# Moving one of the three softmax-sum additions of a layer-1 attention group from VectorE to an accumulating DMA issued by GpSimd

## Chip, cores and metric

The kernel runs on one core of one Trainium2 chip. The metric is the device time of one execution in microseconds (us). Three runs of the kernel before took 2781.45, 2784.82 and 2786.3 us; the median is 2784.82 us.

## What is computed

Two gated layers work on x of shape 8 x 512 x 256 with a context of 8 x 512 x 128. Each layer adds a gated attention part and a gated feed-forward part to x. The change touches the attention of layer 1, which has two blocks, a1 (self, with a mask on the normalised probabilities) and a2 (cross, on keys and values of the context):

```python
q = jnp.einsum('bsc,hcd->bhsd', xn, wq)      # H=16 heads, D=32
k = jnp.einsum('btc,hcd->bhtd', yn, wk)
v = jnp.einsum('btc,hcd->bhtd', yn, wv)
a = jax.nn.softmax(jnp.einsum('bhsd,bhtd->bhst', q, k) * D ** (-0.5), axis=-1)
if causal:
    mask = (jnp.arange(t)[None, :] > jnp.arange(s)[:, None]).astype(a.dtype)
    a = a * mask
o = jnp.einsum('bhst,bhtd->bhsd', a, v)
...
x_out = x + o @ li1_w + li1_b
h = jax.nn.gelu(_ln(x_out, ln3_g, ln3_b) @ li2_w + li2_b, approximate=False)
return x_out + h @ li3_w + li3_b
```

The softmax denominator runs over all 512 keys, also in block a1, since the mask comes after the softmax. All of this is in float32.

## The kernel before

Layer 0 fills about the first 920 us of the profile. After it, one woven section holds both attention blocks of layer 1 for all eight sequences, their MLPs (`mlp1`), the projections of queries and keys (`pair1`), the norms that enter a block (`pre1`, `enter1`), the last part of layer 0's feed-forward (`first`) and layer 1's feed-forward (`last`, `tail`).

**The attention steps.** `steps1` makes the list of one block: 4 groups `g` of 4 heads, and in each group 4 key tiles `n` of 128 keys. With 8 sequences and 2 blocks that is 64 groups and 256 steps. A step has two halves.

- `front(g, n)`: TensorE multiplies keys by queries into two PSUM tiles `ps_s`; ScalarE takes the exponential of both into one SBUF tile `pt` (128 keys x 4 heads x 512 queries, float32, 1 MB; L2217). In block a1 GpSimd makes a masked copy `dg` of the diagonal piece (L2221).
- `back(g, n)`: TensorE multiplies `pt` (and `dg`) by the values `vt` into the PSUM tile `ov`. For n = 1, VectorE makes `acc` = pt(0) + pt(1) (L2246). For n = 2, `acc` gets pt(2) as well (L2248). For n = 3, TensorE multiplies a matrix of ones by `acc` and by pt(3) into `sm`, which gives the denominators; VectorE turns them into reciprocals (`rt`, `recs`, `rb`, L2261 to L2264) and scales `ov` into `oT` (L2266).

`pt` has three buffers (`PTS = 3`), `acc` one, `dg` two, `ov` one. pt(n) of a group is freed when the additions and matmuls that read it are done; pt(2)'s buffer is next written by the front of n = 1 of the following group.

**The order.** `weave_all` merges the 256 steps with nine chains of other work. A front may be at most two ahead of the backs:

```python
if self.fronts < len(steps) and self.fronts - self.backs < 2:
```

A planner (`Pace`) keeps a model of when each engine is free and each tile is done, and `weave_all` emits the piece with the lowest place in the order among those that can start on TensorE within 0.3 us of the modelled present. The order is so fixed when the program is built; each engine then works through its own queue in that order. The back of n = 3 waits in the model until `acc` is done:

```python
return max(t, pace.when([Pace.name(st["acc"])]), pace.place("m1")) if n == NT - 1 else t
```

The model gives a two-input VectorE operation 0.15 us + 0.00106 us an element, so 2.3 us for `acc`. A DMA it models so (bytes n):

```python
self.free[e] = t0 + 0.4
self.wire = max(self.wire, t0 + 1.2) + n / 280e3
end = self.wire + 1.2
```

Where a piece can go to ScalarE or VectorE, `pace.sooner` chooses by the modelled load of the two.

Of the kernel before, what the change touches and what calls it, by code (L numbers as in the profile page):

```python
# [11 lines left out]
ALU = mybir.AluOpType  # L12
# [939 lines left out]
class Fast(General):  # L952
# [1238 lines left out]
    def steps1(self, b, blk):  # L2191
# [3 lines left out]
        nc, work, q, pace = self.nc, self.work, self.seqs[b], self.pace  # L2195
# [3 lines left out]
        st = {}  # L2199
# [29 lines left out]
        def back(g, n):  # L2229
            self.backs += 1  # L2230
            kt, pt, parts = st.pop((g, n))
            if n == 0:
                st["ov"] = self.ovp.tile([P, T], F32, tag="ov1", name="ov")
            ov = st["ov"]
            for i, (p, cols) in enumerate(parts):
                for j in (2, 3, 0, 1):
                    h = 4 * g + j
                    self.mm(
                        ov[32 * j : 32 * j + 32, cols], q["vt", blk][:, kt, 32 * h : 32 * h + 32],
                        p[:, j, : cols.stop - cols.start],  # L2240
                        n == 0 and i == 0, n == NT - 1 and i == len(parts) - 1,
                    )

            if n == 1:
                st["acc"] = work.tile([P, 4, T], F32, tag="acc", name="acc")
                nc.vector.tensor_tensor(st["acc"], st["pt"], pt, ALU.add)  # L2246
            elif n == 2:
                nc.vector.tensor_tensor(st["acc"], st["acc"], pt, ALU.add)  # L2248
            st["pt"] = pt
            if n < NT - 1:  # L2250
                return
            sm = self.bank()
            for k, t in enumerate((st["acc"], pt)):
                for j in (2, 3, 0, 1):
                    self.mm(sm[32 * j : 32 * j + 32, :], self.ones, t[:, j, :], k == 0, k == 1)

            if g == 0:
                st["recs"] = work.tile([P, 4, 16], F32, tag="recs", name="recs", bufs=2)
            rec = st["recs"][:, g, :]
            rt = work.tile([P, 16, 32], F32, tag="rt", name="rt", bufs=1)  # L2260
            nc.vector.transpose(rt.rearrange("p b d -> p (b d)"), sm)  # L2261
            nc.vector.reciprocal(rec, rt[:, :, 0])
            rb = work.tile([P, T], F32, tag="rt", name="rb", bufs=1)
            nc.vector.transpose(rb, rec.unsqueeze(2).to_broadcast([P, 16, 32]))  # L2264
            oT = q["oT", blk, g] = work.tile([P, T], F32, tag="oT", name="oT", bufs=5)
            nc.vector.tensor_tensor(oT, ov, rb, ALU.mult)  # L2266
            if g == 3:
                self.seen(st["recs"])

        def back_at(g, n):  # L2270
# [5 lines left out]
            if n == 0:  # L2276
# [3 lines left out]
        return [  # L2280
            (lambda g=g: front_at(g), lambda g=g, n=n: back_at(g, n),
             lambda g=g, n=n: front(g, n), lambda g=g, n=n: back(g, n))
            for g in range(4) for n in range(NT)
        ]
# [317 lines left out]
```

## Time and profile before

| | |
|---|---|
| median of three runs | 2784.82 us (2781.45 to 2786.3) |
| span of the profiled execution | 2779.7 us; the runs' median is 5.1 us more |
| mean granted TensorE clock | 0.959 |
| TensorE (PE) busy | 2517.8 us, 91% |
| VectorE (DVE) busy | 1736.5 us, 62% |
| ScalarE (ACT) busy | 1452.2 us, 52% |
| GpSimd (POOL) busy | 614.8 us, 22% |
| L2246, `acc` = pt(0) + pt(1) | 64 instructions, 149.2 us |
| L2248, `acc` += pt(2) | 64 instructions, 149.4 us |
| DMA queue of GpSimd | 2.62 MB in the whole program, none in layer 1's attention |

The time of the profiled execution itself is not given apart from its span, so the 5.1 us is taken for what lies around the span. In the profile a line such as `L2248 DVE TENSOR_TENSOR acc<-acc,pt` names the source line, the engine, the operation and the tiles written and read. `L1053` is the helper that records every matmul, so matmuls are told apart by their tiles: `ps_s` are the scores, `ov` the products with the values, `ps<-acc,ones` the first half of the denominators. "Idle before" is the time in which an engine stood still ahead of an instruction, with what released it. PEld is TensorE's weight load.

### The profile page before, as it was taken

What the parts mean: (1) busy time and instruction counts of PE and PEld (TensorE: products, weight loads), DVE (VectorE), ACT (ScalarE), POOL (GpSimd) and SP (SyncE); (2) the same over time, 40 slices, a digit from 0 to 9 for tenths busy, and PEclk for the clock granted to TensorE, in tenths of its full rate; (3) what the DMA queues carried; (4) which work ended last, traced back from release to release, by engine and by line L of the source; (5) the groups of instructions that cost most, each with busy time, mean ns of one, the idle gap of its engine ahead of it and who ended that gap; (6) DMA issues with size and microseconds to landing.
All of it is one profiled execution on the core that took longest, in us unless ns stands there. A gap on an engine that the chain in (4) does not pass through costs nothing.

```text
span 2779.7 us, 38478 instructions
## 1 busy us (share of the span) xinstructions
PE 2517.8 (91%) x15447; PEld 1223.8 (44%) x15452; DVE 1736.5 (62%) x3135; ACT 1452.2 (52%) x1803; POOL 614.8 (22%) x682
## 2 busy tenths in 40 slices
PE   7999999999786989999999999988999989999875
PEld 2333333333233344535554535545455454454554
DVE  4544554343476666564666777676777877767766
ACT  4666666656573554445444455444554555555421
POOL 2212222111001344231334231111114332101100
PEclk9999999999886999999999999999999999999987
DMA  3001120000364512211211013211021102211010
GB/s 113 25 27 50 50 73 16 20 31 12 118 261 173 178 46 99 80 46 42 76 60 63 16 54 107 69 38 58 24 82 60 43 4 89 71 45 43 23 38 17
DMA packets 76475, 176.55 MB, mean 64 GB/s; under 512 B 7424, under 2 KB 36480, under 8 KB 68992
## 3 DMA queue, kind: packets, MB, share of 16 engines
q1 hardware_dynamic: 73904, 170.81, 17.6%
q8 instruction: 123, 2.02, 0.3%
q0 software_dynamic: 800, 2.62, 0.3%
q10 hardware_dynamic: 1584, 0.58, 0.1%
q14 instruction: 64, 0.52, 0.1%
HBM read 111.07 MB, written 62.91 MB: 63 GB/s over the span
## 4 chain that ended last, share of the span: by engine, by line
PE 46%; DVE 13%; ACT 4%; POOL 2%; issue 2%; DMA 0%; ACTq 0%; POOLq 0%; DVEq 0%; SPq 0%
PE ps L1053 31%; PE ps_s L1053 8%; PE ov L1053 6%; ACT pt L2217 2%; PE ps L1056 1%; DVE hF L2332 1%; DVE acc L2246 1%; POOL dg L2221 1%; DVE rb L2264 1%; DVE hm L2342 1%; DVE z L144 1%; DVE mv L1971 1%; DVE rt L2261 1%; DVE oT L2266 1%; DVE acc L2248 1%
## 5 line engine op out<-in xcount | busy, mean ns | idle before, releaser
L2217 ACT ACTIVATE pt<-ps_s 128x1024 f32<-128x1024 f32 x512 | 496.3, 1021 | 418.0 <-PE ps_s L1053 313.6
L1053 PE MATMUL ps_s<-QT,KT 32*128 32x512 f32 (+3 forms) x4096 | 613.2, 607 | 28.3 <-ACT pt L2217 16.1
L1431 ACT ACTIVATE pt<-ps_s 128x1024 f32<-128x1024 f32 (+3 forms) x512 | 411.2, 862 | 202.6 <-PE ps_s L1053 194.3
L1053 PEld LDWEIGHTS ps_s<-QT,KT 32*128 32x128 f32 x4096 | 191.6, 184 | 368.0 <-issue 201.8
L1053 PE MATMUL ps<-x3T,li 128*128 128x256 f32 x1024 | 244.9, 391 | 3.9 <-DVE hp L2320 2.4
L1053 PE MATMUL ov<-pt,v 128*32 128x512 f32 (+3 forms) x2048 | 232.7, 525 | 13.5 <-POOL pt L1434 12.7
L1053 PE MATMUL ps<-li,hD 128*128 128x256 f32 x1024 | 239.1, 389 | 5.7 <-ACT hD L2164 5.7
L1053 PE MATMUL ov<-pt,vt 128*32 128x512 f32 (+3 forms) x1792 | 204.4, 526 | 36.2 <-DVE oT L2266 29.4
L1977 POOL TENSOR_SCALAR mv<-mv 128x2 f32<-128x2 f32 (+1 forms) x105 | 57.7, 550 | 770.4 <-DVE mv L1972 735.3
L2221 POOL TENSOR_SCALAR_AFFINE_SELECT dg<-pt 128x512 f32<-128x512 f32 x128 | 116.1, 908 | 505.6 <-ACT pt L2217 505.4
L1053 PEld LDWEIGHTS ps<-x3T,li 128*128 128x128 f32 x1024 | 192.5, 194 | 60.7 <-issue 18.4
L1053 PEld LDWEIGHTS ps<-li,hD 128*128 128x128 f32 x1024 | 193.8, 194 | 56.4 <-issue 14.5
L1434 POOL TENSOR_SCALAR_AFFINE_SELECT pt<-pt 128x512 f32<-128x512 f32 x128 | 86.3, 674 | 471.7 <-ACT pt L1431 470.0
L2248 DVE TENSOR_TENSOR acc<-acc,pt 128x2048 f32<-128x2048 f32 x64 | 149.4, 2334 | 4.3 <-ACT pt L2217 3.2
L2246 DVE TENSOR_TENSOR acc<-pt 128x2048 f32<-128x2048 f32 x64 | 149.2, 2332 | 1.1 <-ACT pt L2217 1.1
L1456 DVE STREAM_TRANSPOSE ot<-ov 128x512 f32<-128x512 f32 x64 | 45.8, 716 | 165.9 <-PE ov L1053 165.9
L2332 DVE SCALAR_TENSOR_TENSOR hF<-hp,cols,hF 128x256 f32<-128x256 f32 x224 | 114.6, 512 | 41.7 <-ACT hF L2323 35.6
L1053 PE MATMUL ps<-zT,a_wq 128*128 128x512 f32 x256 | 127.8, 623 | 2.1 <-DVE zT L2058 2.1
L1053 PE MATMUL ps<-li,oT 128*128 128x256 f32 x512 | 128.0, 394 | 1.7 <-DVE oT L2266 1.0
L1759 ACT ACTIVATE hD<-ps,cols 128x256 f32<-128x256 f32 x123 | 54.7, 471 | 137.1 <-PE ps L1053 100.5
L1053 PEld LDWEIGHTS ov<-pt,v 128*32 128x32 f32 x2048 | 40.4, 108 | 167.1 <-issue 100.2
L1053 PEld LDWEIGHTS ps<-li,oT 128*128 128x128 f32 x512 | 92.9, 191 | 47.7 <-issue 16.1
(305 smaller groups left out, 3654.9 us busy)
## 6 DMA issues: line engine op xcount, KB each, us to landing
hd<-h SPq DMA_DIRECT2D x16, 1024.0 KB, 3.9
hF<-hd SPq DMA_DIRECT2D x16, 1024.0 KB, 6.7
li<-in_w_a_dram SPq DMA_DIRECT2D x12, 1024.0 KB, 5.0
fw<-q_f_w SPq DMA_DIRECT2D x22, 512.0 KB, 5.5
xF<-xd SPq DMA_DIRECT2D x22, 512.0 KB, 5.1
kd<-k SPq DMA_DIRECT2D x8, 1024.0 KB, 3.9
vd<-v SPq DMA_DIRECT2D x8, 1024.0 KB, 5.2
res<-rd SPq DMA_DIRECT2D x32, 256.0 KB, 2.8
```

The costliest lines, as they stand in the source:

```text
L144: self.nc.vector.tensor_scalar(out[:, i, :], x[:, i, :], mv[:, i, 0:1], rstd[:, i : i + 1], ALU.subtract, ALU.mult,)
L1053: self.nc.tensor.matmul(out, lhsT, rhs, start=start, stop=stop, skip_group_check=True)
L1431: nc.scalar.activation(pt[:, 2 * jp : 2 * jp + 2, lo:], pss[jp][:, :, lo:], AF.Exp)
L1434: nc.gpsimd.affine_select(out=diag, in_=diag, compare_op=ALU.is_ge, fill=0.0, base=0, pattern=[[0, 4], [1, P]], channel_multiplier=-1,)
L1456: nc.vector.transpose(ot.rearrange("p b d -> p (b d)"), ov)
L1759: self.nc.scalar.activation(out, ps, AF.Identity, bias=bias)
L1977: nc.gpsimd.tensor_scalar(rstd, mv[:, :, 1], EPS, None, ALU.add)
L2217: nc.scalar.activation(pt[:, 2 * jp : 2 * jp + 2, :], pss[jp], AF.Exp)
L2221: nc.gpsimd.affine_select(out=dg, in_=pt[:, :, diag], compare_op=ALU.is_gt, fill=0.0, base=0, pattern=[[0, 4], [-1, P]], channel_multiplier=1,
L2246: nc.vector.tensor_tensor(st["acc"], st["pt"], pt, ALU.add)
L2248: nc.vector.tensor_tensor(st["acc"], st["acc"], pt, ALU.add)
L2332: nc.vector.scalar_tensor_tensor(a, hp[:, half + k : half + k + n], self.col("conv_w", 3 * f + k), a, ALU.mult, ALU.add)
```

## The change

For n = 2 the addition on VectorE is replaced by a DMA that GpSimd issues; it reads `pt`, adds it to `acc` in SBUF and writes `acc`. Nothing else is edited, and the planner, which models the new instruction as a DMA, orders the section anew.

```diff
--- before.py
+++ after.py
@@ -2245,7 +2245,7 @@
                 st["acc"] = work.tile([P, 4, T], F32, tag="acc", name="acc")
                 nc.vector.tensor_tensor(st["acc"], st["pt"], pt, ALU.add)
             elif n == 2:
-                nc.vector.tensor_tensor(st["acc"], st["acc"], pt, ALU.add)
+                nc.gpsimd.dma_start(st["acc"], pt, accum_op=ALU.add)
             st["pt"] = pt
             if n < NT - 1:
                 return
```

## Prediction

> **What bounds the kernel now.** I read the busy shares first, then the chain, then the stage that the change touches, then single groups. The page:
>
> ```profile
> PE 2517.8 (91%) x15447; PEld 1223.8 (44%) x15452; DVE 1736.5 (62%) x3135; ACT 1452.2 (52%) x1803; POOL 614.8 (22%) x682
> PE 46%; DVE 13%; ACT 4%; POOL 2%; issue 2%; DMA 0%; ACTq 0%; POOLq 0%; DVEq 0%; SPq 0%
> L2248 DVE TENSOR_TENSOR acc<-acc,pt 128x2048 f32<-128x2048 f32 x64 | 149.4, 2334 | 4.3 <-ACT pt L2217 3.2
> ```
>
> TensorE is the busiest engine and has the largest share of the chain; VectorE is second. The row of the edited line says that 64 additions of 2.33 us are removed. From the windows view, the stage that holds all 64 groups:
>
> ```profile
> core 0: us, PE busy (x) PEld busy (x) DVE busy (x) ACT busy (x) POOL busy (x), PEclk, DMA share, GB/s
> 925.00:2615.00 1690.00, 1581.01 (x9758) 827.60 (x9754) 1167.25 (x1997) 848.61 (x1000) 440.33 (x446) 0.97 0.18 59
> ```
>
> Of 1690 us TensorE is idle for 109. So emptying VectorE can bring at most these 109 us, and each microsecond that TensorE waits anew is to be paid unless it takes the place of a wait already there. The average group has 1690 / 64 = 26.4 us. The chain in this stage gives L2248 1.0% (17 us), L2246 1.8%, and `dg` 1.6% (27 us). What TensorE and ScalarE wait for, from the waits view of the stage:
>
> ```profile
> PE ov L1053 <- DVE oT L2266: 29.4, 18, 4.9
> PE ps L1053 <- DVE acc L2248: 4.7, 3, 2.3
> ACT pt L2217 <- DVE acc L2246: 56.1, 28, 4.9
> ```
>
> L2248 itself stops TensorE little (4.7 us). ScalarE's 56 us are for L2246, which frees pt(0) and stays. Then how soon the sum is needed, in one pressed group of the timeline:
>
> ```profile
> 976.01 2.29 DVE L2246 TENSOR_TENSOR acc<-pt 128x2048 f32<-128x2048 f32 x1 [0.58 <-ACT pt L2217]
> 976.11 2.69 POOL L2221 TENSOR_SCALAR_AFFINE_SELECT dg<-pt 128x512 f32<-128x512 f32 x1 [2.50 <-ACT pt L2217]
> ...
> 983.92 2.28 DVE L2248 TENSOR_TENSOR acc<-acc,pt 128x2048 f32<-128x2048 f32 x1
> ...
> 986.26 1.94 PE L1053 MATMUL ps<-acc,ones 128*32 128x512 f32 x8 [2.32 <-DVE acc L2248]
> ```
>
> The `acc` matmul starts 0.06 us after L2248 ends and TensorE stood idle 2.32 us for it. I took two distances from the timeline for all 64 groups. From the end of L2248 to the first `acc` matmul: median 3.9 us, below 1.1 us in 16 groups. From the end of L2246, when the new transfer could start at the earliest (pt(2) is mostly done by then), to that matmul: median 9.9 us, 20 groups below 7.0, 30 below 8.8, 40 below 12.0.
>
> **What the Trainium skill says.** "DMA: Bandwidth & Descriptors", section "Anatomy of one DMA — SWDGE (gpsimd) path", prices a GpSimd DMA at 2.0 us + bytes/436e3, thus 4.4 us for a plain 1 MB. The trace is slower: its only GpSimd loads of 256 KB took 4.3 us where this gives 2.6. I use the trace. The same page, section "Rules for kernel authors", says that an accumulating DMA reads its destination and writes it later; no page gives a rate for that, and nothing in this trace shows one. "SBUF — State Buffer", section "Who interferes with whom", says that a VectorE instruction with two SBUF inputs blocks a GpSimd instruction that reads SBUF. The trace agrees: the `dg` above started 0.1 us into L2246 and took 2.69 us, against a median of 0.635.
>
> **The change, part by part.** *Removed:* 64 x 2.334 = 149.4 us of VectorE. Most lies beside TensorE's work. On the path there were 17 us of L2248 itself. GpSimd's blocking by L2248 goes too: the 128 `dg` are 908 ns on average against 635, half of the surplus put to L2248 (the other half to L2246), so 27 us x 0.273/0.908 / 2 = 4 us. Together 21, taken as **20 us of gain**. Bounds: 0 (something else in VectorE's queue, such as `z`, is late next) and 40 (the reciprocals behind L2248, L2261 to L2266, move up as well).
>
> *Added: a transfer's latency.* The nearest rows:
>
> ```profile
> hd<-h SPq DMA_DIRECT2D x16, 1024.0 KB, 3.9
> vt<-vd SPq DMA_DIRECT2D x8, 1024.0 KB, 4.8
> rd<-res SPq DMA_DIRECT2D x16, 256.0 KB, 2.0
> res<-rd SPq DMA_DIRECT2D x32, 256.0 KB, 2.8
> cT<-cd POOLq DMA_DIRECT2D x8, 256.0 KB, 4.3
> ```
>
> Between 256 KB and 1 MB lie 1.9 to 2.0 us, so 1 MB moves in about 2.6. A plain 1 MB from GpSimd would land 4.3 + 1.9 = 6.2 us after issue. Reading the destination as well adds 2.6: **8.8 us is my value**, 5.2 of it data and 3.6 fixed. Bounds: 5.0 (the fastest `cT` load, 3.1, plus 1.9, the second read hidden) and 14.0 (the adding halves the data rate again: 3.6 + 10.4).
>
> *Where it falls.* The planner knows the transfer: 1.2 + 1,048,576/280e3 + 1.2 = 6.15 us. It holds back(3) until then; that half-step begins with `ov` matmuls (0.4 to 1.0 us), so a pressed group will be laid out with 7.0 us from ready operands to the `acc` matmul. The old order shows that the plan is kept: planned 2.3 us, measured 2.34 to 3.35 in the 16 pressed groups. So:
> 1. The 20 groups below 7.0 us lack 36 us of distance in all, which the planner fills with other TensorE work (MLPs, projections). It is scarce in the first groups, which follow each other at 13 to 16 us; I take a quarter unfilled: **9 us lost** (bounds 0 and 36).
> 2. The transfer lands 1.8 us after the planned 7.0: 20 x 1.8 = 36 us. Ten more groups between 7.0 and 8.8 lack 7 us. TensorE works in order, so it stands for these 43 us, while VectorE and ScalarE catch up and later waits (the 109 us) shrink. I take a quarter off: **32 us lost**.
>
> *Other parts.* GpSimd gets 64 issues of about 0.54 us (the `cT` issue), 35 us on an engine busy 440 of 1690. In its queue the DMA stands behind `dg` of step 3 and ahead of `dg` of the next group's first step, and it waits for L2246. Behind it are that `dg` and the norm operations (L1977, L1978); but the next `dg` needs an exponential that comes later still. Zero; without that cover, a norm is late by what L2246 lags, 1 to 2 us in some groups. SP's queue is not passed. The engines of the DMA are busy 18% of the stage; 64 x 5.2 us adds 333/1690 = 20 points. TensorE waits for a load almost nowhere (`vt`, 1.7 us), so nothing is charged. pt(2)'s buffer is held until landing, but its next writer comes after back(3) on TensorE, which waits for the same landing: zero. After back(3), `oT` is as much later as the sum, and the next group's `ov` needs its buffer; a pressed group can't be shorter than about 19 us (12.8 us at the least now, and 6 more), still under the average of 26.4.
>
> Sum: 9 + 32 - 20 = **+21 us**. Against the profiled execution: 2779.7 of span plus 5.1 around it, which is the median of 2784.8; thus 2806.
>
> **Rivals.**
> - *The landing is hidden: faster.* If the transfer lands within the planned 7.0 us, nothing is lost but the filling: 9 - 20 = -11, thus 2774; at best -40, 2745. It decides at the landing where the lost time equals the gain: (late sum) x 0.75 + 9 = 20, a late sum of 15 us, which is a landing of 7.7 us. For it speaks the 6.2 us of a plain transfer; against it the second read and that `cT` took up to 8.1 us.
> - *The adding is slow.* At a landing of 12 us the late sum is 154 us (40 groups): 115 + 9 - 20 = +104, thus 2889; at 14, +168, 2953. No line speaks for or against a rate.
> - *GpSimd's queue becomes the bound*, if writing the descriptors takes far longer than 0.54 us or the DMA's wait holds the norms: 2 us in each of 64 groups, half of it seen by TensorE, is 64 us on top of -11, thus 2838. GpSimd is idle three quarters of the stage, which speaks against it.
> - *The change does little as ordered anew.* The planner sends more pieces to the emptier VectorE and lays out the whole section otherwise; a shift of 5 us either way would hide a small effect, thus 2780 to 2790.
>
> **How the numbers follow.** About 0.2% (5.6 us) is what a measurement of this kernel can tell from no change. Landing at 7.8 to 10.5 us: 0.42, its own range 2785 to 2850. Hidden: 0.36, 2745 to 2785. Slow adding: 0.13. GpSimd's queue: 0.05. Little: 0.04. Faster gets most of the hidden case, 0.35 in all; the parts of the first two cases around zero and the last give 0.11; slower 0.54. The range 2760 to 2875 leaves out some 0.08 below and 0.11 above.
>
> **What would show it.** The median time from the DMA's issue to its landing (8.8; below 7.7 the sign turns). TensorE's wait for `acc`, now 4.7 us from L2248, should be 30 to 60 us, put to the DMA. VectorE's busy time should fall by about 149 us, `dg`'s mean to some 770 ns, and the shortest distance from L2246's end to the `acc` matmul should rise from 2.45 to about 8. I am wrong if `acc` matmuls wait and the time still falls: then other waits were worth more than I took, or if nothing waits and the time rises: then the new order or GpSimd's queue costs it.

## The result, and the profile after

The changed kernel took 2927.64 us (median of 4 runs, 2917.7 to 2930.18), against 2783.14 us before on the same chip: a ratio of 1.0513, 95% interval 1.0492 to 1.0533, or 144 us slower. The forecast was 2806 us, range 2760 to 2875: the direction was right, the size was not. The span of the profiled execution is 2925.5 us. From the page (busy times, then groups with busy time and mean, then the issue with its time to landing):

```profile
PE 2563.1 (88%) x15452; PEld 1232.1 (42%) x15452; DVE 1585.7 (54%) x3073; ACT 1458.0 (50%) x1816; POOL 607.2 (21%) x746
L2221 POOL TENSOR_SCALAR_AFFINE_SELECT dg<-pt 128x512 f32<-128x512 f32 x128 | 95.3, 745 | 586.5 <-ACT pt L2217 586.5
L1053 PE MATMUL ps<-acc,ones 128*32 128x512 f32 x512 | 80.2, 702 | 95.0 <-DMA acc<-pt 88.5
L2248 POOL DMA_DIRECT2D acc<-pt x64 | 58.7, 916 | 462.2 <-DVE acc L2246 128.1
acc<-pt POOLq DMA_DIRECT2D x64, 1024.0 KB, 7.6
```

VectorE is 151 us less busy (1736.5 to 1585.7), the masked copies became shorter (908 to 745 ns), and the transfer lands 7.6 us after its issue, sooner than the 8.8 us of the prediction. Still TensorE waits 88.5 us for it. The windows view of the attention stage, which now ends at 2760 instead of 2615 us:

```profile
core 0: us, PE busy (x) PEld busy (x) DVE busy (x) ACT busy (x) POOL busy (x), PEclk, DMA share, GB/s
925.00:2760.00 1835.00, 1631.43 (x9766) 839.72 (x9765) 1020.33 (x1942) 857.73 (x1018) 433.03 (x510) 0.95 0.35 91
```

All of the loss is in this stage: it is 145 us longer. TensorE's idle time rose from 109 to 204 us. Its busy time rose by 50 us for the same matmuls. Part of this is the granted clock, whose mean fell from 0.97 to 0.95. The clock is either full or half in the trace; inside the stage the half-clock spells add up to 85 us before and 174 us after. TensorE was at work in 78 and 136 us of them, and half of the difference, 29 us, is work lost. Counted at full clock the matmuls still take 21 us more, 16 of them in the scores (`ps_s`); why the new order has that is not shown.

One masked group of the timeline shows what the new addition has to wait for:

```profile
1564.22 2.28 DVE L2246 TENSOR_TENSOR acc<-pt 128x2048 f32<-128x2048 f32 x1
...
1566.59 1.94 ACT L2217 ACTIVATE pt<-ps_s 128x1024 f32<-128x1024 f32 x2 [0.68 <-DVE acc L2246]
...
1568.66 0.63 POOL L2221 TENSOR_SCALAR_AFFINE_SELECT dg<-pt 128x512 f32<-128x512 f32 x1 [0.43 <-ACT pt L2217]
1569.25 0.93 POOL L2248 DMA_DIRECT2D acc<-pt  x1
...
1577.77 1.94 PE L1053 MATMUL ps<-acc,ones 128*32 128x512 f32 x8 [3.32 <-DMA acc<-pt]
```

L2246 ends at 1566.50. It frees the buffer of pt(0), and only then can ScalarE write pt(3) into it; the masked copy of pt(3) stands ahead of the DMA in GpSimd's queue. So the DMA leaves 2.75 us after both of its operands were ready, and lands 11 us after L2246. Over the 64 groups the DMA starts 2.76 us (median) after L2246 ends. This median hides two kinds: 4.0 us in the 32 masked groups, 0.74 us in the 32 cross groups, which have no masked copy. Of TensorE's 88.5 us of waiting, 69.8 us fall in the masked groups.

### The profile page after: what moved, and what is told of

The parts are those of the page before. It is cut to its first block, busy times and chain, and to the rows that moved or that the text cites. A ratio compares the mean times of both kernels' runs of the same rounds, so it can differ in the third digit from the quotient of the medians.

```text
span 2925.5 us, 38659 instructions
## 1 busy us (share of the span) xinstructions
PE 2563.1 (88%) x15452; PEld 1232.1 (42%) x15452; DVE 1585.7 (54%) x3073; ACT 1458.0 (50%) x1816; POOL 607.2 (21%) x746
## 4 chain that ended last, share of the span: by engine, by line
PE 31%; DVE 8%; DMA 6%; ACT 3%; issue 2%; POOL 1%; POOLq 0%; ACTq 0%; SPq 0%; DVEq 0%
PE ps L1053 22%; DMA acc<-pt 5%; PE ps_s L1053 5%; PE ov L1053 3%; ACT pt L2217 1%; DVE hF L2332 1%; DVE acc L2246 1%; DVE rb L2264 1%; DVE rt L2261 1%; PE ps L1056 1%; DVE oT L2266 1%; ACT hD L2164 0%; DVE hm L2342 0%; DVE hp L2320 0%; POOL mv L1977 0%
## 5 line engine op out<-in xcount | busy, mean ns | idle before, releaser
L1053 PE MATMUL ps_s<-QT,KT 32*128 32x512 f32 (+3 forms) x4096 | 633.9, 613 | 24.9 <-ACT pt L2217 20.0
L1053 PEld LDWEIGHTS ps_s<-QT,KT 32*128 32x128 f32 x4096 | 199.7, 187 | 386.1 <-issue 223.4
L1053 PE MATMUL ps<-li,hD 128*128 128x256 f32 x1024 | 242.3, 391 | 12.9 <-ACT hD L2164 12.8
L1053 PE MATMUL ov<-pt,v 128*32 128x512 f32 (+3 forms) x2048 | 232.7, 525 | 13.5 <-POOL pt L1434 12.7
L1053 PE MATMUL ps<-x3T,li 128*128 128x256 f32 x1024 | 240.8, 391 | 1.1 <-ACT x3T L2140 0.9
L1053 PE MATMUL ov<-pt,vt 128*32 128x512 f32 (+3 forms) x1792 | 203.0, 523 | 33.7 <-DVE oT L2266 23.0
L1053 PEld LDWEIGHTS ps<-li,hD 128*128 128x128 f32 x1024 | 193.6, 194 | 74.4 <-ACT hD L2164 20.9
L2221 POOL TENSOR_SCALAR_AFFINE_SELECT dg<-pt 128x512 f32<-128x512 f32 x128 | 95.3, 745 | 586.5 <-ACT pt L2217 586.5
L1053 PEld LDWEIGHTS ps<-x3T,li 128*128 128x128 f32 x1024 | 195.4, 195 | 49.3 <-issue 13.2
L1053 PE MATMUL ps<-acc,ones 128*32 128x512 f32 x512 | 80.2, 702 | 95.0 <-DMA acc<-pt 88.5
L2248 POOL DMA_DIRECT2D acc<-pt x64 | 58.7, 916 | 462.2 <-DVE acc L2246 128.1
L2246 DVE TENSOR_TENSOR acc<-pt 128x2048 f32<-128x2048 f32 x64 | 150.4, 2350 | 2.8 <-ACT pt L2217 2.8
L2261 DVE STREAM_TRANSPOSE rt<-ps 128x512 f32<-128x512 f32 x64 | 45.8, 715 | 157.6 <-PE ps L1053 157.4
L1053 PE MATMUL ps<-zT,a_wq 128*128 128x512 f32 x256 | 126.2, 616 | 3.1 <-DVE vt L2030 2.3
L1053 PE MATMUL ps<-li,oT 128*128 128x256 f32 x512 | 125.0, 389 | 0.7 <-DVE oT L2266 0.5
L1761 DVE TENSOR_SCALAR hD<-ps,cols 128x256 f32<-128x256 f32 x134 | 62.0, 481 | 103.6 <-PE ps L1053 78.9
```

The costliest lines, as they stand in the source:

```text
L1053: self.nc.tensor.matmul(out, lhsT, rhs, start=start, stop=stop, skip_group_check=True)
L1761: self.nc.vector.tensor_scalar(out, ps, bias, None, ALU.add)
L2221: nc.gpsimd.affine_select(out=dg, in_=pt[:, :, diag], compare_op=ALU.is_gt, fill=0.0, base=0, pattern=[[0, 4], [-1, P]], channel_multiplier=1,
L2248: nc.gpsimd.dma_start(st["acc"], pt, accum_op=ALU.add)
```

## The experiments

Two theories were set against each other at first. LATE: the sum lands after TensorE wants it. ORDER: the order that the planner lays out for a slow sum is worse in itself. ORDER was later split into HOLD (the loss comes from holding back the last half-step, and grows with the delay) and LUCK (any order laid out anew fits less well than the old one, whatever the delay). Lines added to a kernel shift its line numbers: L1053 becomes L1057 or L1066 in some views, L2266 becomes L2267 or L2272. Only the edit at the addition is shown below; the few lines of the planner's model that it needs are left out.

**The new order with VectorE's addition.** In front of the addition the planner is told to take it for a DMA of GpSimd (`pace.recast` replaces engine, operation and sources in its model):

```diff
-                nc.gpsimd.dma_start(st["acc"], pt, accum_op=ALU.add)
+                pace.recast = ("Pool", "DMACopy", [pt[:]])
+                nc.vector.tensor_tensor(st["acc"], st["acc"], pt, ALU.add)
+                pace.recast = None
```

> The order of the changed kernel, instruction for instruction, but the third addition is done by VectorE at its place (the planner is told that it is a DMA from GpSimd). Theory LATE (the cost is that the sum lands after TensorE wants it, in this order or in the old one): without the landing the new order costs little, 2770 to 2815 us. Theory ORDER (the planner's new order is itself worse, because it holds back the denominators and runs out of other work): most of the 144 us stays, over 2860 us.

Measured 2884.67 us, ratio 1.0358 (1.0341 to 1.0376), +102 us. ORDER holds: 102 us stay with no transfer at all. Half-clock spells in the stage: 154 us. TensorE's waits grew in many places at once, none of them for the sum. From the waits view (us in total, times, longest), first the kernel before, then this run; the wait for `oT` was 29.4 us before:

```profile
PE ps L1056 <- ACT z L1983: 1.0, 2, 0.8
PE ov L1053 <- DVE mv L1981: 3.8, 2, 3.6
PE ps L1053 <- ACT hD L2164: 2.4, 5, 0.7
```

```profile
PE ps L1060 <- ACT z L1987: 18.7, 17, 4.6
PE ov L1057 <- DVE mv L1985: 14.8, 7, 4.3
PE ps L1057 <- ACT hD L2168: 12.8, 6, 2.9
PE ov L1057 <- DVE oT L2272: 39.3, 20, 9.6
```

One thing keeps the 102 us from being the price of the order alone: the planner laid this order out for a VectorE that is 149 us emptier, and here VectorE does the additions all the same.

**The old order with the DMA.**

```diff
+                pace.recast = ("DVE", "TensorTensor", [st["acc"][:], pt[:]])
                 nc.gpsimd.dma_start(st["acc"], pt, accum_op=ALU.add)
+                pace.recast = None
```

> The order of the kernel before, instruction for instruction, but with the accumulating DMA in place of the third addition (the planner is told that it is VectorE's addition). Theory LATE: in the old order the sum is wanted 9.9 us (median) after the second addition ends; the DMA leaves up to 2.8 us after that and lands 7.6 us later, so at 10.4 us about 130 us are late in all, and the stalls bring half-clock spells: 2900 to 2970 us. Theory ORDER: the old order kept, the loss is at most half of the changed kernel's, under 2855 us.

Measured 2983.5 us, ratio 1.0726 (1.0708 to 1.0744), +201 us, a little above what LATE gave. The two theories are thus both true, of two different orders: the old order can't bear the landing, and the new one costs 102 us before there is any. TensorE's longest wait in the stage, from the waits view:

```profile
PE ps L1057 <- DMA acc<-pt: 175.8, 31, 11.4
```

Here the half-clock spells come to 242 us, 157 more than before. Much of them falls on the waits themselves: TensorE's busy time rose by 40 us for the same matmuls in the same order, so about 40 of the 201 us are clock.

**The third addition left out, old order.** The addition is not emitted; a call in its place charges the planner's model with it as before.

```diff
-                nc.vector.tensor_tensor(st["acc"], st["acc"], pt, ALU.add)
+                pace.pretend(st["acc"], pt)
```

> The order of the kernel before with the third addition left out altogether (pt of the third key tile is missing from the denominators; the planner still counts it), so VectorE is 149 us emptier and nothing takes the place of the addition. The prediction's step of 20 us of gain gives 2764 us, its bounds 2744 to 2784. If VectorE's relief is worth nothing on TensorE's path: 2780 to 2786.

Measured 2765.21 us, ratio 0.994 (0.9924 to 0.9957), 18 us faster. In the old order an emptier VectorE is worth about what the prediction said.

**The DMA issued early.** A function `third(g)` issues the DMA as soon as front(2) and back(1) are both emitted; it is called at the end of `front` and after L2246.

```diff
+            third(g)
+        def third(g):
+            if st.get("summed") == g or (g, 2) not in st or (g, 1) in st or self.backs <= 16 * slot + 4 * g + 1:
+                return
+            st["summed"] = g
+            nc.gpsimd.dma_start(st["acc"], st[g, 2][1], accum_op=ALU.add)
...
-            elif n == 2:
-                nc.gpsimd.dma_start(st["acc"], pt, accum_op=ALU.add)
+                third(g)
```

> The changed kernel, but the accumulating DMA is issued as soon as both the second addition and the third front are emitted, so ahead of the fourth front's masked copy in GpSimd's queue; the planner orders anew. Theory LATE with the GpSimd queue as part of it (in the masked blocks the DMA leaves 2.8 us after the second addition ends, since it stands behind a masked copy that itself waits for that addition and an exponential): the 2.8 us go, TensorE's wait for the DMA at least halves, 2810 to 2870 us. Theory ORDER: still 2890 us or more. If the queue does not matter: 2915 to 2935 us.

Measured 2875.93 us, ratio 1.0343 (1.0322 to 1.0364): 52 us less than the changed kernel, just above the range that LATE with the queue gave. The DMA now starts 0.54 us (median) after L2246, and TensorE waits 50.7 us for it instead of 88.5, not quite half less:

```profile
PE ps L1053 <- DMA acc<-pt: 50.7, 24, 4.7
```

Since the planner laid out another order here, the same was done in the fixed old order:

**The DMA issued early, old order.** `third(g)` as above, hidden from the planner, with the `pretend` call at n = 2.

> The order of the kernel before on TensorE, VectorE and ScalarE, with the DMA in place of the third addition and issued early, as in the run of the early issue; the planner knows nothing of it. Theory LATE with GpSimd's queue: the sum is ready 8.1 us after the second addition ends instead of 10.4, the late sum of the old distances falls from 130 to 59 us, so against the 200 us lost without the early issue about half: 2860 to 2890 us. If GpSimd's queue does not matter here: over 2950 us.

Measured 2897.8 us, ratio 1.0406 (1.0381 to 1.043), a little above the 2890 us that LATE gave. Against the 2983.5 us of the old order with the DMA in its place, 86 us are gone by moving one instruction in one queue:

```profile
PE ps L1066 <- DMA acc<-pt: 92.8, 26, 8.2
```

So the place in GpSimd's queue is a real part of the lateness: 175.8 us of waiting become 92.8. Nearly all of the fall is in the masked groups (137.5 to 62.9 us; cross groups 38.3 to 29.9).

**The planner told of a later sum, VectorE adding.** Only this line is added to the kernel before, with 3 and with 6 us:

```diff
                 nc.vector.tensor_tensor(st["acc"], st["acc"], pt, ALU.add)
+                pace.done[pace.name(st["acc"])] += 3
```

> The kernel before, VectorE doing the third addition as before; only the planner is told that each sum is done 3 us later than it takes it to be. Theory HOLD (holding back a group's last half-step by itself lengthens the run, since no more than two fronts may be ahead and the other work runs out): a loss that grows with the delay, here 20 to 50 us, 2803 to 2833. Theory LUCK (any new order costs some tens of us against a well fitted one, whatever the delay): a loss that does not follow the delay, the same here as with 6 us. No cost from holding: 2780 to 2790.

Measured 2815.71 us, ratio 1.0106 (1.0085 to 1.0127), +32 us.

> As the run before it, with 6 us instead of 3. Theory HOLD: at least double the loss of 3 us, 60 to 120 us, 2843 to 2903. Theory LUCK: within 20 us of the run with 3 us.

Measured 2865.88 us, ratio 1.0283 (1.0261 to 1.0306), +82 us. VectorE does every addition as before; only the order differs, and with it the choice of ScalarE or VectorE for some pieces (ScalarE has 1826 instructions with 6 us, 1803 before). The loss follows the delay, at the two delays tried, as HOLD says and LUCK does not. Where some of it sits is seen in TensorE's waits with 6 us:

```profile
PE ov L1053 <- DVE oT L2267: 50.5, 27, 4.3
PE ps L1056 <- DVE z L144: 25.7, 19, 4.3
```

The first was 29.4 us in 18 waits before, the second 14.9. Once the denominators of a group come late, the next group's first `ov` matmul meets the chain from the denominators to `oT`, which frees its buffer.

**Early issue, and a planner that knows.** The planner is told that the transfer also waits for `acc`, and to add 2.65 instead of 1.2 us at its end, 7.6 us in all.

> The early issue of the DMA, and the planner is told the truth: that the transfer waits for the second addition and lands 7.6 us after its issue. Theory LATE part: TensorE's wait for the DMA (50.7 us with the early issue alone) falls under 20 us. Under HOLD the time does not fall by as much, as the groups are held back longer: 2850 to 2880 us; if the waits were the whole cost left, 2800 to 2830 us.

Measured 2840.5 us, ratio 1.0191 (1.0167 to 1.0215). The time was a little under the range of HOLD; the wait fell less than expected:

```profile
PE ps L1057 <- DMA acc<-pt: 33.2, 15, 4.5
```

It is the best of the versions that transfer the whole sum in all groups, but still 57 us slower than VectorE's addition. Two things were told at once, so which of them helped is not separated.

**Half of the transfer, and a copy.** Both keep the changed kernel's order (`pace.recast` stands around the edited line as above).

```diff
-                nc.gpsimd.dma_start(st["acc"], pt, accum_op=ALU.add)
+                nc.gpsimd.dma_start(st["acc"][:, 0:2, :], pt[:, 0:2, :], accum_op=ALU.add)
```

> The changed kernel in its own order, but the DMA adds only heads 0 and 1 of each group (512 KB; for heads 2 and 3 the third key tile is missing from the denominators). It prices the transfer by size. If the data part of the 7.6 us is what the prediction took (5.2 us for 1 MB), the landing falls to 5.0 us; if the transfer is mostly fixed time, it stays above 6.3.

```diff
-                nc.gpsimd.dma_start(st["acc"], pt, accum_op=ALU.add)
+                nc.gpsimd.dma_start(st["acc"], pt)
```

> The changed kernel in its own order, but the DMA copies the third tile into the sum instead of adding it (the first two key tiles are missing from the denominators). It prices the adding. If the second read costs what the prediction took (2.6 us), the landing falls from 7.6 to 5.0 us; if adding costs nothing, it stays at 7.6.

One run each: 2855.91 and 2850.0 us. The issues, first of the half, then of the copy:

```profile
acc<-pt POOLq DMA_DIRECT2D x64, 512.0 KB, 5.0
```

```profile
acc<-pt POOLq DMA_DIRECT2D x64, 1024.0 KB, 4.9
```

Half a megabyte lands 2.6 us sooner, so on a straight line through the two sizes 1 MB of adding has 5.2 us of data time and 2.4 of fixed time. The adding costs 7.6 - 4.9 = 2.7 us over a copy. These two runs also price the step from 5 to 7.6 us of landing in the new order: with 5 us it is 72 to 78 us faster than the changed kernel (one run each, so to some us only). They do not price all of the lateness, since TensorE still waits for the transfer, first the half, then the copy:

```profile
PE ps L1057 <- DMA acc<-pt: 26.5, 11, 5.1
```

```profile
PE ps L1057 <- DMA acc<-pt: 33.0, 12, 5.2
```

**The third addition left out, planner knowing.**

```diff
-            elif n == 2:
-                nc.vector.tensor_tensor(st["acc"], st["acc"], pt, ALU.add)
```

> The third addition left out (the third key tile is missing from the denominators), and here the planner knows, so it lays out a new order on a VectorE that is 149 us emptier; no result is ever late. Theory LUCK in the small: a new order by itself costs something against the old one, so 2775 to 2800, above the 2765 of the old order without the addition. If a new order costs nothing by itself: 2755 to 2770.

Measured 2784.07 us, ratio 1.0011 (0.9995 to 1.0027). An order laid out anew costs some 19 us against the old order without the addition, although nothing is late. In the two profiled executions, 30 us apart, 18 us are matmul time counted at full clock, 16 of it in the scores. That is LUCK in the small.

**The change in the cross blocks only.** In the masked blocks VectorE adds as before.

```diff
-            elif n == 2:
+            elif n == 2 and strict:
+                nc.vector.tensor_tensor(st["acc"], st["acc"], pt, ALU.add)
+            elif n == 2:
                 nc.gpsimd.dma_start(st["acc"], pt, accum_op=ALU.add)
```

> The change in the 32 groups of the cross blocks only, where no masked copy stands ahead of the DMA in GpSimd's queue; the masked blocks keep VectorE's addition. If the loss is shared evenly by groups: 72 us, 2855. If the queue behind the masked copy is a large part, the cross blocks take clearly less than half: 2800 to 2835.

Measured 2847.54 us, ratio 1.0226 (1.0205 to 1.0247), +63 us. Half of the groups, without any masked copy, bring 44% of the loss, nearer to an even share (2855 us) than to the other case (2800 to 2835). In the changed kernel the masked groups have most of the waiting for the transfer, but the cross groups alone lose 63 us without a masked copy: in the order that the planner chose, the queue behind the masked copy is not what most of the loss depends on.

## Why the prediction was right or wrong, point by point

**The gain.** 20 us was forecast (0 to 40) and 18 measured in the old order. The agreement is in part luck: in the profiled execution of that run, the fastest of five, the stage is 29 us shorter, and 16 of these are busy time of TensorE, whose half-clock spells fell from 85 to 58 us. The prediction had no term for the clock.

**The transfer.** 8.8 us was forecast, 7.6 measured. What adding costs over a copy (2.6 forecast, for the second read; 2.7 measured) and the data time (5.2, 5.2) were right; the fixed part was 2.4, not 3.6. The 4.3 us of `cT`, on which it rested, were not the only GpSimd loads of 256 KB: two of `w` took 5.9 us (median), further off still. By the prediction's own turning point of 7.7 us, this landing should have made the kernel no slower. That it lost 144 us shows that the failure lies in the other terms.

**Step 1, the filling, failed.** It put 9 us (at most 36) on holding back the last half-step, on the view that a quarter of the missing distance would find no filler. With VectorE adding and the sum never late, telling the planner 3 and 6 us later costs 32 and 82 us, and the changed kernel's own order costs 102. The distance that was to be filled was summed over the 20 groups below 7.0 us, as if the other 44 would keep their places. But holding moves everything that follows: the median distance from L2246's end to the `acc` matmul went from 9.9 us to 12.3 in the new order with VectorE adding (13.1 in the changed kernel, where waiting for the landing is part of it). That two fronts are the limit, so that no attention work can pass a held half-step, is an argument from the code: a looser limit was not tried, so this cause is not shown. How much of the 102 us is the holding, how much a new order that fits less well, and how much VectorE's additions, for which this order left no room, is not separated either; the 19 us of the order without an addition is one measure of the second.

**Step 2, the lateness, was less than half of what it was.** 32 us was forecast; the step from a landing of 5 us to one of 7.6 alone measured 72 to 78, with 26 to 33 us of waiting left at 5 us. Three things were left out. First, "In its queue the DMA stands behind `dg` of step 3" was noted and charged with zero, since only what waits behind the DMA was priced. What the DMA waits behind was a cost: from L2246's end to the landing it is 10.8 us at the median, not 7.6, and in the old order moving the DMA ahead of that copy was worth 86 us.

Second, the planner does not lay out "7.0 us from ready operands". Of the DMA's operands its model waits for pt(2) alone; that the DMA also waits for `acc`, and so for L2246, is not in it. L2246 ended after pt(2) was written in 51 of the 64 groups of the changed kernel, and 2.55 us after it at the median of all. In the same order with VectorE adding, 8 groups still have less than 7.0 us from L2246's end to the `acc` matmul.

Third, a stall was taken at less than its length (a quarter off) for waits that shrink later. The Trainium skill, "TensorE: Matmul & The Clock Gate", section "What's actually happening", says that TensorE falls to half clock after an idle window of about 3.4 us. The trace agrees on the step: the half-clock spells are 3.4 us long or multiples of it. It does not show that a single wait must be so long: of the 17 spells in the stage before, only 2 have a wait of over 3.4 us in the 8 us ahead of them; ahead of the other 15 the longest was 0.9 to 3.2 us. Where TensorE waits most there are most of the spells (85 us before, 174 in the changed kernel, 242 in the old order with the DMA). In the new order 62 and 56 us less of waiting for the transfer (the half and the copy) went with 72 and 78 us less time. Taken together, a stall here cost more than its length, not less.

**The sum.** The new order cost 65 to 71 us with a landing of 5 us, VectorE's relief included, where the prediction had 9 - 20 = -11; the rest of the landing cost 72 to 78, where it had 32. That these two make the 144 us is no proof of its own, as it is one difference cut in two. The half and the copy are 29 to 35 us under VectorE's addition in the same order; this is what VectorE's relief is worth there, less what TensorE still waits for the transfer. The clock's 29 us are inside these terms, not beside them.

**The rivals.** The hidden landing did not happen: 7.6 us from the issue is near the 7.0 that it needed, but from L2246's end it is 10.8, and TensorE waited 88.5 us. Slow adding is excluded by the 2.7 us. GpSimd's queue mattered by its order, not by the issue: 0.92 us each, where 0.54 was taken from a load and the plain copy took 0.60. "The change does little as ordered anew" had a right place, the planner's new order, with the wrong size: a few us there; in the runs 19 with no addition to place, 102 in the changed kernel's order.

**The signs named.** VectorE fell by 151 us (149 forecast), `dg` to 745 ns (some 770), the shortest distance rose to 7.6 us (about 8). TensorE's wait for the DMA was 88.5 us, above the 30 to 60.

## What to carry to other kernels

Before an operation goes to a slower path, ask when its result is wanted and count from ready operands to landing, with everything that stands ahead of it in the new queue and what that in turn waits for. Where a planner lays out the order by modelled times, a longer latency changes the order of everything, and that can cost as much as the wait; keep the order and change the operation, then keep the operation and change the order, to see the two apart. Where TensorE is nearly always busy, a stall can cost more than its length, because the clock may fall with it; read from the trace how short a stall already does so.

## What was not expected of the hardware

An accumulating transfer of 1 MB inside SBUF needs 0.92 us of GpSimd for its issue against 0.60 for the same transfer as a plain copy, and it lands 2.7 us later than the copy (7.6 and 4.9 us). While it ran 64 times, the share of the DMA engines in the stage went from 0.18 to 0.35, with no wait for another transfer showing among TensorE's longest. Other transfers did land later (`vt` 5.7 us instead of 4.8, `xP` 5.9 instead of 5.0).
